# A two-layer graph network: layer 0's PSUM banks and query buffers lent to the last stretch of layer 1, and the tables of a batch group made four tiles further ahead

## The chip, the cores and the metric

The kernel runs on one core of a Trainium2 chip. The metric is the device time of one execution in microseconds. Before the change it is 2400.64 us, the median of three runs (2385.87 to 2404.24). The core has five instruction queues that run side by side: TensorE (PE, with its weight loads PEld), VectorE (DVE), ScalarE (ACT), GpSimd (POOL) and SyncE (SP). PE writes into PSUM[...]. POOL and SP mostly issue DMAs here: SP the plain ones, POOL those that gather or scatter rows by a list of indices.

## The reference, cut to what matters

x has 8 batches of 2048 nodes with 256 features; adj is a symmetric 0/1 matrix with about nine neighbours in a row, the node itself among them.

```
# layer 0: chunked attention, 4 heads of 64, chunks of 256 nodes
scores = clip(q . k / 8, -10, 10);  scores = -10 where adj == 0
attn   = softmax within each chunk;  ctx = attn @ v, summed over the 8 chunks
x = layernorm(x + LN(ctx @ Wo.T + x))
# layer 1: graph attention, 4 heads of 64
Wh = x @ W;  e = leaky_relu(s_src[i] + s_dst[j], 0.2), -inf where adj == 0
x = layernorm(x + elu(softmax(e over j) @ Wh))
```

Since adj has few ones, the kernel works on neighbour lists. Where adj is 0, a score in layer 0 is exactly -10, so all these together come to a constant part that the sum of v over a chunk supplies.

## The kernel before, in words

**Lists.** `edge_lists` reads adj in 16 tiles of 128 nodes, finds for each node its neighbours (at most 24), sorts all nodes by their number of neighbours, scatters the records in that order to `rec_d` (L118, POOL) and reads them back as `srt` (L122, SP). A tile of sorted nodes then needs as many slots as its largest node: `CAPS`, from 24 down to 5. `node`, `idx` and `valid` come out of `srt`. While it works, it calls `between(it)` after each tile of adj, which makes one table tile of batch group 0.

**Tables.** The 8 batches go in four groups g of two. `tables(g, t)` computes for 128 nodes of both batches k and v (into `kv_d[g]`, one DRAM row of 4 KB a node) and q (into `qx_d[g]`, beside x). Every second tile it loads two tiles of x (`load_x`, SP), transposes them on PE into `tk` banks (L336), copies them out with ACT, and hands the pair before to `add_beta` (POOL, L351, followed by SP's write to `qx_d`). Group g is complete after 16 table tiles, the last of which also makes the group's bias.

**Layer 0.** For tile t of group g, `fetch0` issues one indirect DMA on POOL for each slot: it gathers for each of the 128 nodes the `kv_d` row of its neighbour (L489). Two slots are a unit, and units come from a ring of 14 buffers (`RING`). Another gather brings `qx` (L527). `scores0` multiplies and sums, `softmax0` normalises, `context0` weights the v parts in place (L501 on DVE, L507 on ACT for a quarter of the units) and sums the slots on PE by transposing them into one PSUM bank `acc` (L514). `finish0` multiplies by Wo and applies both layernorms, and `rows1` makes layer 1's row (Wh and the logits of both batches) for `wh_d`.

**Layer 1** works on two groups together (p = 0 for groups 0 and 1, p = 1 for groups 2 and 3), so that its rows in `wh_d[p]` are 4160 bytes. `fetch1` gathers them, also through L489. `softmax1` (L680 to L700) needs all slots of the tile and leaves the weights in the SBUF tile `e`. `context1` weights both groups' parts in place (L501 and L507 again) and sums them into two `acc` banks, which ACT copies out (L722). `finish1` transposes back through the single `mf` bank (L734), applies elu (L737 to L741) and the layernorm, and leaves a `scatter` in the list `late`: for p = 0 one indirect DMA to `hold_d` (L748), for p = 1 four to the output (L753), which POOL issues when `scatters()` is called.

**Order.** `seq` is the order of all tiles, written out by hand: 32 tiles of layer 0 (groups 0 and 1), then two tiles of layer 0 (groups 2 and 3) for each tile of layer 1 with p = 0, and last the 16 tiles of layer 1 with p = 1, with nothing beside them. I call these the last stretch. In step k the loop first issues the gathers of step k + 1 (`fetch`), then the scatters, then scores, the earlier tiles' `rows1` and `finish0`, one table tile of the next group, and this tile's softmax and context. Before the first tile of a new group, `tables_first` holds the fetch back until the last table of that group has been made, because any row of the group may be gathered. The framework below places the instructions on each engine's queue in an order of its own near the written one, and puts in the waits. Each engine then works strictly in its queue's order.

**PSUM.** The eight banks are `acc` (2), `tk` (2), `tf` (2), `mf` (1) and `pr` (1). `tk`, `tf` and `pr` are used by layer 0 and its tables; `rows1` also takes `tf`. `qx` has four buffers in SBUF, and layer 1's `xr`, with the same size, two of its own.

Of the kernel before, what the change touches and what calls it, by code (L numbers as in the profile page):

```python
# [9 lines left out]
F32 = mybir.dt.float32  # L10
# [4 lines left out]
ALU = mybir.AluOpType  # L15
# [27 lines left out]

def edge_lists(tc: tile.TileContext, pool, bank, adj, const, ident, rec_d, B, between):

# [49 lines left out]
        between(it)  # L97


    rank = const.tile([P, NT], F32, name="rank")  # L100
    rank_i = pool.tile([P, NT], I32, name="rank_i")

    half = NT // 2
# [4 lines left out]
    for it in range(half):  # L108
        gt = pool.tile([P, N], F32, tag="v", name="v", bufs=2)
        nc.vector.tensor_scalar(gt, krow, key[:, it:it + 1], 0.0, op0=ALU.is_gt, op1=ALU.add,  # L110
                                accum_out=rank[:, it:it + 1])
        junk = pool.tile([P, N], BF16, tag="junk", name="junk", bufs=1)
        k = half + it
        nc.scalar.activation(junk, krow, AF.Sign, bias=nkey[:, k:k + 1], accum_out=rank[:, k:k + 1])
        nc.vector.tensor_scalar(rank[:, k:k + 1], rank[:, k:k + 1], 0.5, 0.5 * (N - 1), op0=ALU.mult, op1=ALU.add)
        nc.vector.tensor_copy(rank_i.rearrange("p (h t) -> p t h", h=2)[:, it], rank.rearrange("p (h t) -> p t h", h=2)[:, it])
        for k in (it, half + it):
            nc.gpsimd.indirect_dma_start(out=views[k],  # L118
                                         out_offset=bass.IndirectOffsetOnAxis(ap=rank_i[:, k:k + 1], axis=0),
                                         in_=rec[:, k, :], in_offset=None)  # L120
    srt = pool.tile([P, NT, REC], F32, name="srt")
    nc.sync.dma_start(srt, rec_d.rearrange("(t p) r -> p t r", p=P))  # L122

# [46 lines left out]
    return idx, valid, same, node, nodeb, rank, over  # L170


@with_exitstack
def sparse_path(ctx: ExitStack, tc: tile.TileContext, keep, x, adj, Wq, bq, Wk, bk, Wv, bv, Wo, bo, gamma, beta, W, a,
# [57 lines left out]
    def bank(tag, bufs=2):  # L232

        return ps.tile([P, 512], F32, tag=tag, name=tag, bufs=bufs)
# [182 lines left out]
        tables(0, t)  # L417


    rings, turn = [ctx.enter_context(tc.tile_pool(name="ring0", bufs=1))], [0]  # L420

    def unit():
# [8 lines left out]

    with tc.tile_pool(name="lists", bufs=1) as pool:
        with nc.allow_low_precision("exact small integers"):
            idx, valid, same, node, nodeb, rank, over = edge_lists(tc, pool, bank, adj, const, ident, rec_d, B,
                                                             first_tables)
        nc.vector.tensor_copy(keep, over)

    rings.append(ctx.enter_context(tc.tile_pool(name="ring1", bufs=1)))
# [57 lines left out]
    def weighted(part, al, s0, n):  # L496

        e = part.shape[2] // D
        pv = part.rearrange("p s (e d) -> p s e d", d=D)
        av = al[:, :, s0:s0 + n].rearrange("p e s -> p s e").unsqueeze(3).to_broadcast([P, n, e, D])  # L500
        nc.vector.tensor_tensor(pv, pv, av, op=ALU.mult)  # L501
# [165 lines left out]
        nc.sync.dma_start(wh_d[g // 2][t * P:(t + 1) * P, g % 2 * WW:(g % 2 + 1) * WW], wh)  # L667


    got1, st1 = {}, {}  # L670

    def fetch1(p, t):
# [2 lines left out]
    def softmax1(p, t):  # L675
        S = CAPS[t]
        units = got1[p, t]
        z = small.tile([P, 2, GH, S], F32, tag="z1", name="z1")
        for u, s0, n in units:
            nc.vector.tensor_tensor(z[:, :, :, s0:s0 + n].rearrange("p k e s -> p s k e"),  # L680
                                    u.rearrange("p s (k w) -> p s k w", k=2)[:, :, :, GF:GF + GH],
                                    sd[p % 2][:, t].unsqueeze(1).to_broadcast([P, n, 2, GH]), op=ALU.add)
# [12 lines left out]
        r = small.tile([P, 2 * GH], F32, tag="r", name="r")  # L695
        nc.vector.tensor_reduce(r, e, axis=AX.X, op=ALU.add)

        nc.vector.tensor_scalar(r, r, 1e-30, None, op0=ALU.max)
        nc.vector.reciprocal(r, r)
        nc.vector.tensor_tensor(e, e, r.unsqueeze(2).to_broadcast([P, 2 * GH, S]), op=ALU.mult)  # L700
        st1[p, t] = e

    def context1(p, t):
        S = CAPS[t]
        e = st1.pop((p, t))
        units = got1.pop((p, t))
        accs = [bank("acc").rearrange("p (c r) -> p c r", r=P) for _ in range(2)]
        na = len(units) // 4, (len(units) + 2) // 4
        for i, (u, s0, n) in enumerate(units):
            for k in range(2):  # L710
                if i >= len(units) - na[k]:
                    weighted_act(u[:, :, k * WW:k * WW + GF], e[:, k * GH:(k + 1) * GH], s0, n)
        for i, (u, s0, n) in enumerate(units):
            for k in range(2):
                part = u[:, :, k * WW:k * WW + GF]
                if i < len(units) - na[k]:
                    weighted(part, e[:, k * GH:(k + 1) * GH], s0, n)
# [6 lines left out]
        xr = work.tile([P, 2, GF], F32, tag="xr", name="xr")  # L724
        nc.sync.dma_start(xr, x1_d[p][t * P:(t + 1) * P])
        st1[p, t] = hTs, xr

    def finish1(p, t):
        hTs, xr = st1.pop((p, t))
        sums = small.tile([P, 2 * G], F32, tag="sums1", name="sums1")  # L730
        for k, hT in enumerate(hTs):
            ph = bank("mf", 1)
            for c in range(G * KC):
                nc.tensor.transpose(ph[:, c * P:(c + 1) * P], hT[:, c, :], ident)  # L734

# [551 lines left out]
```

## Time and profile before

| | |
|---|---|
| median of three runs | 2400.64 us (2385.87 to 2404.24) |
| profiled execution | 2397.55 us, its span 2395.8 us |
| PE, PEld busy | 1900.4 us (79%), 1622.0 us (68%) |
| DVE busy | 1833.5 us (77%) |
| ACT busy | 1409.0 us (59%) |
| POOL busy | 1505.0 us (63%) |
| DMA | 669.10 MB, mean 279 GB/s; indirect DMAs of POOL 505.01 MB |
| granted TensorE clock, mean | 0.885 |
| L489, POOL's gathers | 656 of `kv_d`, mean 1235 ns; 328 of `wh_d`, mean 1270 ns |

An engine's busy time counts its own work, not its waits, and not the time between two DMA issues. In a row of a group stand the line, the engine, the operation, what is written and read, the shapes, how often, then the busy time and the mean of one, and at last the engine's idle time just before these instructions, with what ended it. In a timeline a row has the start, the duration, the engine and the line, and in brackets the idle time before it and its releaser. PEclk is the share of full clock that PE was granted. Times within the execution are counted from the start of its span. By them, the lists and group 0's tables take the first 195 us, the first tile of layer 0 gathers from 195, and the last stretch gathers from 1994 to the end.

### The profile page before, as it was taken

What the parts mean: (1) busy time and instruction counts of PE and PEld (TensorE: products, weight loads), DVE (VectorE), ACT (ScalarE), POOL (GpSimd) and SP (SyncE); (2) the same over time, 40 slices, a digit from 0 to 9 for tenths busy, and PEclk for the clock granted to TensorE, in tenths of its full rate; (3) what the DMA queues carried; (4) which work ended last, traced back from release to release, by engine and by line L of the source; (5) the groups of instructions that cost most, each with busy time, mean ns of one, the idle gap of its engine ahead of it and who ended that gap; (6) DMA issues with size and microseconds to landing.
All of it is one profiled execution on the core that took longest, in us unless ns stands there. A gap on an engine that the chain in (4) does not pass through costs nothing. (4 is left out here: it accounts for less than half of the span.)

```text
span 2395.8 us, 38844 instructions
## 1 busy us (share of the span) xinstructions
PE 1900.4 (79%) x11946; PEld 1622.0 (68%) x11946; DVE 1833.5 (77%) x4099; ACT 1409.0 (59%) x5036; POOL 1505.0 (63%) x1230
## 2 busy tenths in 40 slices
PE   7686889889899898999988885888678786664764
PEld 5565677778778787777876774776566675554653
DVE  6864587877588988588988886887788887775775
ACT  4573455546566555655565665664356677665766
POOL 3125455672666676376668856774677685787883
PEclk9897899899999999999998997987878987877887
DMA  7737877795889798598879977896679896786884
GB/s 259 242 137 272 265 270 281 260 346 209 316 287 320 260 334 319 212 388 298 302 258 353 360 281 238 285 321 221 230 274 326 306 319 248 278 310 231 302 296 154
DMA packets 239982, 669.10 MB, mean 279 GB/s; under 512 B 43688, under 2 KB 70059, under 8 KB 237719
## 3 DMA queue, kind: packets, MB, share of 16 engines
q0 software_dynamic: 156800, 505.01, 60.1%
q1 hardware_dynamic: 79248, 151.55, 17.2%
q10 hardware_dynamic: 3718, 9.97, 1.3%
q8 instruction: 98, 1.61, 0.3%
q14 instruction: 118, 0.96, 0.1%
HBM read 612.79 MB, written 126.36 MB: 309 GB/s over the span
## 5 line engine op out<-in xcount | busy, mean ns | idle before, releaser
L489 POOL DMA_INDIRECT u<-kv_d,idx x656 | 810.2, 1235 | 436.4 <-PE acc L514 185.7
L514 PE MATMUL acc<-ident,u 128*128 128x128 f32 x5248 | 713.4, 291 | 157.0 <-DVE u L501 89.0
L514 PEld LDWEIGHTS acc<-ident,u 128*128 128x128 f32 x5248 | 637.5, 151 | 220.7 <-DVE u L501 133.2
L489 POOL DMA_INDIRECT u<-wh_d,idx x328 | 416.5, 1270 | 148.2 <-issue 76.4
L566 PE MATMUL pr<-ident,u 128*128 128x128 f32 (+1 forms) x1984 | 287.0, 295 | 78.7 <-DVE u L547 77.2
L501 DVE TENSOR_TENSOR u<-u,al 128x1024 f32<-128x1024 f32 x280 | 334.5, 1234 | 1.5
L566 PEld LDWEIGHTS pr<-ident,u 128*128 128x128 f32 (+1 forms) x1984 | 245.4, 151 | 110.8 <-DVE u L547 104.6
L547 DVE TENSOR_TENSOR u<-u,qx 128x1024 f32<-128x1024 f32 (+1 forms) x248 | 302.0, 1218 | 18.3 <-DMA u<-kv_d,idx 15.1
L501 DVE TENSOR_TENSOR u<-u,z 128x1024 f32<-128x1024 f32 x266 | 314.4, 1212 | 0.6
L507 ACT ACTIVATE u<-u,z 128x64 f32<-128x64 f32 x1008 | 262.0, 337 | 25.0 <-DVE z L700 17.1
L507 ACT ACTIVATE u<-u,al 128x64 f32<-128x64 f32 x800 | 209.1, 342 | 23.2 <-DVE al L607 22.3
L663 PE MATMUL mf<-wa,x1T 128*128 128x264 f32 x512 | 167.6, 455 | 23.1 <-ACT x1T L658 14.8
L351 POOL TENSOR_TENSOR xt<-xt,beta_r 128x1024 f32<-128x1024 f32 x32 | 77.1, 2410 | 143.1 <-PE tk L336 126.3
L385 PE MATMUL tk<-wq,xT 128*128 128x256 f32 x512 | 145.2, 397 | 24.4 <-ACT kvs L379 24.4
L451 ACT ACTIVATE nm<-sums 128x2 f32<-128x2 f32 (+1 forms) x160 | 32.4, 202 | 221.3 <-DVE sums L641 122.6
L372 PE MATMUL tk<-wkv,xT 128*128 128x256 f32 x512 | 151.7, 410 | 12.9 <-ACT xC L341 12.6
L635 PE MATMUL mf<-wo,cT 128*128 128x256 f32 x512 | 148.4, 415 | 6.3 <-ACT whs L666 5.3
L376 PE MATMUL tk<-wkv,xC 128*128 128x256 f32 x512 | 144.5, 399 | 0.0
L663 PEld LDWEIGHTS mf<-wa,x1T 128*128 128x128 f32 x512 | 101.7, 218 | 59.7 <-ACT x1T L658 23.6
L455 ACT ACTIVATE sq<-o,nm 128x256 bf16<-128x256 f32 x256 | 129.7, 507 | 5.3
L554 DVE TENSOR_TENSOR u<-u,qx 128x1024 f32<-128x1024 f32 (+1 forms) x96 | 116.0, 1214 | 16.6 <-DMA qx<-qx_d,node 7.1
L590 DVE TENSOR_SCALAR sc<-tf 128x64 f32<-128x64 f32 (+5 forms) x64 | 14.0, 218 | 138.2 <-PE tf L576 138.2
(168 smaller groups left out, 3254.0 us busy)
## 6 DMA issues: line engine op xcount, KB each, us to landing
kv_d<-kvs SPq DMA_DIRECT2D x48, 512.0 KB, 6.0
wh_d<-whs SPq DMA_DIRECT2D x64, 260.0 KB, 5.8
xt<-in_x_dram SPq DMA_DIRECT2D x64, 256.0 KB, 4.8
qx_d<-xt SPq DMA_DIRECT2D x32, 512.0 KB, 4.4
qx_d<-qs SPq DMA_DIRECT2D x64, 256.0 KB, 5.8
x_d<-o SPq DMA_DIRECT2D x64, 256.0 KB, 5.2
xr<-x_d SPq DMA_DIRECT2D x32, 512.0 KB, 4.9
u<-kv_d,idx POOLq DMA_INDIRECT x656, 6.5
```

The source lines that it names most:

```text
L372: nc.tensor.matmul(pm[:, 0:F], xT[:, b * KC + kc, rows], wkv[:, kc, 0:F], start=(kc == 0), stop=False, skip_group_check=True)
L376: nc.tensor.matmul(pm[:, F:], xC[:, b * KC + kc, rows], wkv[:, kc, F:], start=False, stop=(kc == KC - 1), skip_group_check=True)
L385: nc.tensor.matmul(qb, xT[:, b * KC + kc, rows], wq[:, kc, :], start=(b == 0 and kc == 0), stop=False, skip_group_check=True)
L455: nc.scalar.activation(sq, src[:, k, :], AF.Square, bias=nm[:, k:k + 1], accum_out=m2[:, k:k + 1])
L489: nc.gpsimd.indirect_dma_start(out=u[:, k, 0:width], out_offset=None, in_=table, in_offset=bass.IndirectOffsetOnAxis(ap=idx[:, t, s0 + k:s ...
L501: nc.vector.tensor_tensor(pv, pv, av, op=ALU.mult)
L507: nc.scalar.activation(pe, pe, AF.Copy, scale=al[:, e, s0 + k:s0 + k + 1])
L514: nc.tensor.matmul(acc[:, c, :], part[:, k, c * P:(c + 1) * P], ident, is_transpose=True, start=first and k == 0 and c == 0, stop=last and ...
L547: nc.vector.tensor_tensor(prod.rearrange("p k j (s w) -> p k j s w", w=W8), u[:, :, 0:GF].rearrange("p s (k j w) -> p k j s w", k=UNIT, w=W8),
L566: nc.tensor.matmul(pr[0:n * W8, k, :], prod[:, j // (NJ // UNIT), j % (NJ // UNIT), :], ident, is_transpose=True, start=(j == 0), stop=(j ...
L635: nc.tensor.matmul(po[:, b, :], cT[:, b * KC + kc, :], wo[:, kc, :], start=(b == 0 and kc == 0), stop=False, skip_group_check=True)
L663: nc.tensor.matmul(pw[:, 0:F + 2 * H], xT[:, b * KC + kc, :], wa[:, kc, :], start=(kc == 0), stop=(kc == KC - 1))
```

## The change

- **Tables further ahead.** A new `lead_tables` makes the first four table tiles of group 1. `edge_lists` calls it, through the new argument `behind`, after the records' scatter and before `srt` is read. In the loop, step i of layer 0 now makes the table tile i + 16 + 4 in place of i + 16. So the tables of the last group are written out by step 43 in place of 47. `tables_first` is dropped: the fetch is always the first thing in a step. `rank` is allocated earlier, since group 1's tables store it.
- **Weights in PSUM.** For p = 1 (`LAST`), `softmax1` writes the normalised weights `w` into a `tf` bank, for the units that DVE weights. The slots that ACT weights are still scaled in the SBUF tile `e`, by an instruction of their own. `context1` hands `w` to `weighted` (L501).
- **Banks.** For p = 1, every second tile sums into `mf` and `pr` in place of the two `acc`, and `finish1` transposes into `tk` in place of `mf`.
- **xr** takes `qx` buffers (four) for p = 1.
- **Scatters.** In the last stretch, from its second tile on, `scatters` leaves the newest scatter in the list for one step more.

```diff
+    LEAD = 4
+    def lead_tables():
+        for t in range(LEAD):
+            tables(1, t)
...
             nc.gpsimd.indirect_dma_start(out=views[k],
...
+    behind()
     srt = pool.tile([P, NT, REC], F32, name="srt")
...
+    LAST = NG // 2 - 1
...
-        nc.vector.tensor_tensor(e, e, r.unsqueeze(2).to_broadcast([P, 2 * GH, S]), op=ALU.mult)
-        st1[p, t] = e
+        first = 0
+        if p == LAST:
+            w = bank("tf")[:, 0:2 * GH * S].rearrange("p (e s) -> p e s", s=S)
+            nc.vector.tensor_tensor(w, e, r.unsqueeze(2).to_broadcast([P, 2 * GH, S]), op=ALU.mult)
+            first = UNIT * (len(units) - (len(units) + 2) // 4)
+        else:
+            w = e
+        if first < S:
+            nc.vector.tensor_tensor(e[:, :, first:], e[:, :, first:], r.unsqueeze(2).to_broadcast([P, 2 * GH, S - first]),
+                                    op=ALU.mult)
+        st1[p, t] = w, e
...
-        accs = [bank("acc").rearrange("p (c r) -> p c r", r=P) for _ in range(2)]
+        other = p == LAST and order.index(t) % 2
+        accs = [bank(*((("mf", 1), ("pr", 1))[k] if other else ("acc", 2))).rearrange("p (c r) -> p c r", r=P)
+                for k in range(2)]
...
-                    weighted(part, e[:, k * GH:(k + 1) * GH], s0, n)
+                    weighted(part, w[:, k * GH:(k + 1) * GH], s0, n)
...
+        if p == LAST:
+            xr = work.tile([P, 2, GF], F32, tag="qx", name="xr", bufs=4)
+        else:
+            xr = work.tile([P, 2, GF], F32, tag="xr", name="xr")
...
-            ph = bank("mf", 1)
+            ph = bank("tk") if p == LAST else bank("mf", 1)
...
-    def scatters():
-        for f in late:
-            f()
-        late.clear()
+    def scatters(keep=0):
+        while len(late) > keep:
+            late.pop(0)()
...
-        tables_first = layer == 0 and seq[k + 1][0] == 0 and seq[k + 1][1] % NT == 0
-        if not tables_first:
-            fetch(k + 1)
-        scatters()
+        fetch(k + 1)
+        scatters(int(layer == 1 and g == LAST and i > NT))
...
-            if g + 1 < NG:
-                tables(g + 1, i % NT)
-            if tables_first:
-                fetch(k + 1)
+            if i + NT + LEAD < NG * NT:
+                tables(*divmod(i + NT + LEAD, NT))
```

More of the change, by code (lines that the diff above doesn't have):

```diff
@@ L42, with edge_lists @@
 EMIN = 4.5399929762484854e-05
-def edge_lists(tc: tile.TileContext, pool, bank, adj, const, ident, rec_d, B, between):
+def edge_lists(tc: tile.TileContext, pool, bank, adj, const, ident, rec_d, rank, B, between, behind):
     nc = tc.nc
@@ L97, in edge_lists @@
         between(it)
-    rank = const.tile([P, NT], F32, name="rank")
     rank_i = pool.tile([P, NT], I32, name="rank_i")
@@ L169, in edge_lists @@
     nc.vector.tensor_copy(over, op)
-    return idx, valid, same, node, nodeb, rank, over
+    return idx, valid, same, node, nodeb, over
 @with_exitstack
@@ L417, in first_tables @@
         tables(0, t)
+    LEAD = 4
+    def lead_tables():
+        for t in range(LEAD):
+            tables(1, t)
+    rank = const.tile([P, NT], F32, name="rank")
     rings, turn = [ctx.enter_context(tc.tile_pool(name="ring0", bufs=1))], [0]
@@ L433, in sparse_path @@
         with nc.allow_low_precision("exact small integers"):
-            idx, valid, same, node, nodeb, rank, over = edge_lists(tc, pool, bank, adj, const, ident, rec_d, B,
-                                                             first_tables)
+            idx, valid, same, node, nodeb, over = edge_lists(tc, pool, bank, adj, const, ident, rec_d, rank, B,
+                                                             first_tables, lead_tables)
         nc.vector.tensor_copy(keep, over)
@@ L699, in softmax1 @@
         nc.vector.reciprocal(r, r)
-        nc.vector.tensor_tensor(e, e, r.unsqueeze(2).to_broadcast([P, 2 * GH, S]), op=ALU.mult)
-        st1[p, t] = e
+        first = 0
[9 more added lines that the diff above has]
+        st1[p, t] = w, e
     def context1(p, t):
         S = CAPS[t]
-        e = st1.pop((p, t))
+        w, e = st1.pop((p, t))
         units = got1.pop((p, t))
-        accs = [bank("acc").rearrange("p (c r) -> p c r", r=P) for _ in range(2)]
+        other = p == LAST and order.index(t) % 2
+        accs = [bank(*((("mf", 1), ("pr", 1))[k] if other else ("acc", 2))).rearrange("p (c r) -> p c r", r=P)
+                for k in range(2)]
         na = len(units) // 4, (len(units) + 2) // 4
@@ L723, in context1 @@
             hTs.append(hT)
-        xr = work.tile([P, 2, GF], F32, tag="xr", name="xr")
+        if p == LAST:
+            xr = work.tile([P, 2, GF], F32, tag="qx", name="xr", bufs=4)
+        else:
+            xr = work.tile([P, 2, GF], F32, tag="xr", name="xr")
         nc.sync.dma_start(xr, x1_d[p][t * P:(t + 1) * P])
```

## The prediction

> **What bounds the kernel now.** I read the page first (PE 79%, DVE 77%, POOL 63% of the span), saw that no engine bounds the whole, and asked for windows stage by stage. The columns are the stretch, its length, busy us of each engine, the granted clock, the DMA share and GB/s.
>
> ```profile
> core 0: us, PE busy (x) PEld busy (x) DVE busy (x) ACT busy (x) POOL busy (x), PEclk, DMA share, GB/s
> 160.00:360.00 200.00, 154.98 (x855) 129.01 (x854) 123.21 (x255) 96.46 (x306) 109.26 (x97) 0.84 0.74 248
> ...
> 540.00:620.00 80.00, 74.93 (x480) 63.39 (x477) 53.10 (x123) 49.16 (x186) 23.85 (x20) 1.00 0.56 196
> ...
> 1280.00:1400.00 120.00, 100.36 (x675) 86.09 (x675) 97.49 (x213) 75.46 (x278) 97.01 (x73) 0.93 0.95 355
> ...
> 2063.00:2348.00 285.00, 175.57 (x1188) 150.89 (x1188) 199.68 (x458) 188.46 (x679) 228.89 (x184) 0.81 0.78 285
> ```
>
> At the start (160 to 360) nothing is full: PE has 45 us to spare. At the first change of group (540 to 620) DMA falls to 0.56 and POOL all but stops, but PE is 94% busy. Around 1280 to 1400 DMA is at 0.95. In the last stretch no compute engine passes 70%, and POOL shows 80%. The groups of that stretch show what the 80% hides:
>
> ```profile
> L489 POOL DMA_INDIRECT u<-wh_d,idx x132 | 164.4, 1246 | 40.2 <-issue 26.5 <-PE acc L514 5.2 <-DVE u L501 3.4
> ...
> L501 DVE TENSOR_TENSOR u<-u,z 128x1024 f32<-128x1024 f32 x109 | 129.1, 1216 | 0.2
> ...
> L753 POOL DMA_INDIRECT out_dram<-xr,nodeb x52 | 64.5, 1240 | 19.3 <-issue 7.9 <-ACT xr L470 4.3 <-ACT u L507 2.4
> ...
> L738 DVE SCALAR_TENSOR_TENSOR xr<-mf,xr 128x512 f32<-128x512 f32 x22 | 15.1, 686 | 8.5 <-DMA xr<-x_d 5.1 <-ACT hT L737 3.4
> ```
>
> 132 + 52 = 184 indirect DMAs. Each is followed by 0.30 us, so 164.4 + 64.5 + 184 x 0.30 = 284 us of 285: POOL issues without a hole and **is** the bound there; who "released" each 0.30 us is chance. How long one issue takes is in the timeline of two moments of that stretch:
>
> ```profile
> 2191.34 0.24 DVE L680 TENSOR_TENSOR z<-u,sd 128x32 f32<-128x32 f32 x1 [2.85 <-DMA u<-wh_d,idx]
> 2191.53 0.99 POOL L489 DMA_INDIRECT u<-wh_d,idx  x1 [0.30 <-issue]
> 2192.83 1.00 POOL L489 DMA_INDIRECT u<-wh_d,idx  x1 [0.30 <-DMA u<-wh_d,idx]
> ...
> 2225.99 8.02 DVE L501 TENSOR_TENSOR u<-u,z 128x1024 f32<-128x1024 f32 x7
> 2226.04 2.03 POOL L489 DMA_INDIRECT u<-wh_d,idx  x1 [0.30 <-DVE u L501]
> ...
> 2228.38 1.97 POOL L489 DMA_INDIRECT u<-wh_d,idx  x1 [0.31 <-PE acc L514]
> ...
> 2230.65 1.96 POOL L489 DMA_INDIRECT u<-wh_d,idx  x1 [0.30 <-DVE u L501]
> ```
>
> With DVE idle an issue takes 0.99 us; under the multiplications of L501, whose two inputs lie in SBUF, it takes twice that. So DVE sets POOL's pace.
>
> **The last stretch, part by part.** The new factor w makes one input of L501 a PSUM bank in all of the last stretch (133 of the kernel's 266 such instructions). *What POOL gains.* [...] where an input is in PSUM the issue should fall to near 0.99. L680, L741 and the softmax still have two SBUF inputs. In 2050 to 2396 they are some 67 us (L741 24, L680 13, the softmax's lines about 30) against 147 of L501; the excess of 0.25 us on 184 issues, 46 us, shrinks to 67/214 of it, 14 us. That is 1.07 us an issue: 184 x 1.37 = 252 us. POOL gains 32[...].
>
> *What DVE pays.* L738 reads 512 elements from PSUM in 686 ns and L741 256 from SBUF in 410, a slope of 1.08 ns; 1024 elements would take 1239 against 1216. [...] 133 x 0.023 = 3 us by the row[...]. The scaling that stays in SBUF adds 16 small instructions of about 0.25 us (L699 at 128x16 takes 249 ns), 4 us. Both lie in the 85 us that DVE idles in the stretch[...].
>
> *What the stretch then waits for.* DVE needs 200 of 252, ACT 188, PE 176, DMA 0.78 x 285 = 222. All fit, but each tile's softmax needs all its rows landed (DVE waits 61 us at L680), and the ring holds 14 units of which the 24-row tile takes 12: PE idled 20.7 us there while 10 gathers came, and these saw an idle DVE already. So I take 26 of the 32.
>
> *The held-back scatter* removes waits of POOL for ACT's xr, behind which gathers stand: three holes of 3.2, 3.6 and 3.7 us before 2063. The first is not held back; I take 4 of 10. The waits of 13.4 and 8.3 at the end stay, since no gather is behind them. *Accumulators in mf and pr, transposes in tk, xr in the query buffers*: they lift waits of PE (L734 for DVE 37 us, L514 for L722) which POOL's pace covers today; 0, and without that cover they are what lets 26 be reached. Between 0 and 8 us. Last stretch: -30.
>
> **The tables, part by part.** One table tile holds PE from 154.8 to 161.0, 6.2 us, plus half of its pair's 8 transposes (L336), 0.6; ACT 268/64 = 4.2 us. The built order of ACT shows 5 to 6 tables ahead of each context where there were 1 to 2, so the change does what it says. *Front:* some 3.5 more tables come before tile 5 of group 0: 24 us of PE. PE idles 45 us in 160 to 360, partly in places that the in-order queue can't use. POOL now has add_beta of pair 0 in front of the first gather (its transposes ended at 195.1, the gather began at 195.2: +2.4) and that of pair 2 after nine gathers instead of 29; the gathers behind would wait for PE, but they waited for the ring's zeroing until 214 anyway. SP has the x loads and qx_d writes of the pairs behind these. Between 0 and +34; I take +12.
> *Changes of group:* the fetch no longer stands behind the last table.
>
> ```profile
> 580.89 2.42 POOL L351 TENSOR_TENSOR xt<-xt,beta_r 128x1024 f32<-128x1024 f32 x1 [16.23 <-issue]
> 610.09 1.01 POOL L489 DMA_INDIRECT u<-kv_d,idx  x1 [26.78 <-DMA qx_d<-qs]
> ```
>
> POOL's 43 us go (and 44 at 970), but PE was 94% busy, so what returns is PE's 5 us there plus some of the 6 us that it idles in the refill at DMA 1.01 (620 to 660). 0 to 20 each; I take 7. Third change: PE idled 14 us at 1473; 0 to 14, I take 7. *Tiles 43 to 47* lose four tables, 27 us of PE and some 5 MB (256 + 512 + 256 + 256 KB a tile; 14 us at 355 GB/s). The stretch is bound by DMA; 14 is what DMA alone gives, between 0 and 27; I take 13. Tables: +12 - 14 - 7 - 13 = -22.
>
> **Sum.** 2397.55 (span 2395.8) - 30 - 22 = 2345.5 for the profiled execution. That one lies 3.1 below the median of the runs, 2400.64; I state 2348.
>
> **The rivals.**
> *Both parts in full* (0.20). POOL at 0.99 gives 46 + 8, boundaries and tiles 43 to 47 give 40 with the front free: 2397.55 - 94 + 3 = 2307. For: POOL's row has no hole. Against: DVE would run at 84%, DMA at 93% with a 14-unit ring.
> *The pace goes to landing* (0.20). POOL issues faster, but softmax waits for rows and units free no sooner: the tail gives 10 and its scatter 2, the tables 5, because PE at 94% was the bound at the changes of group. 2384. For: PE's 94%, L680's 61 us. Against: at 2186 to 2198 one issue in 1.30 us was followed by landings at that pace.
> *Slower: reading PSUM is dear* (0.09). If a multiplication with its factor repeated from PSUM ran at half pace, 2.43 us, DVE would need 200 + 109 x 1.22 = 333 us in the stretch, more than its 285: DVE is the bound, +63 with some slack, +10 for the 24 others, tables -22: 2452. It decides from 200 + 109 x d = 285, d = 0.78, so 2.0 us an instruction. Against: L738's 686 ns.
> The likeliest case has 0.51, and 2325 to 2372 as its own range.
>
> **Chances and range.** About 1% (24 us) is what a measurement of this kernel tells from no change. Faster: 0.49 of the likeliest, the full case's 0.20, 0.05 of the landing case: 0.74. Same: 0.17, slower: 0.09. Leaving 0.1 at each end gives 2306 to 2392.
>
> **What would show it.** In the changed profile: L489 and L753 of the last stretch at 1.05 to 1.1 us, and the run of 184 issues 25 to 32 us shorter; multiplications out of tf at 1.22 to 1.28 us; POOL's holes of 26.8 and 24.4 us gone, with DMA above 0.75 in those places while PE stays near 94%; the first cT copy (247.4 before) 5 to 20 us later; PE below 80% busy where tiles 43 to 47 are. The prediction is wrong if issues stay near 1.24 us although L501 has one PSUM input, if DVE becomes full in the last stretch, or if the delay of the first tiles is still there at 1400.

## The result, and the profile after

The changed kernel takes 2349.84 us, the median of four runs (2340.43 to 2373.87), against 2393.26 us of the kernel before (2377.1 to 2404.24): a ratio of 0.986, 95% interval 0.982 to 0.990. Here and below a ratio compares only runs that did not fall into the slower of two states, so it can differ a little from the quotient of two medians. The profiled execution has a span of 2350.7 us where before had 2395.8, so 45.1 us are to be found between the two traces. They are easily divided: the gathers of the last stretch began at 1993.8 us before and begin at 1998.0 now, so everything ahead of the last stretch is 4 us *longer*, and the last stretch went from 402 to 353 us, 49 *shorter*. The prediction had -22 and -30 for the two.

The windows that were shown of before, now of after (stretch, its length, busy us of each engine, the granted clock, the DMA share, GB/s); the last is again the part of the last stretch in which POOL shows no hole:

```profile
core 0: us, PE busy (x) PEld busy (x) DVE busy (x) ACT busy (x) POOL busy (x), PEclk, DMA share, GB/s
160.00:360.00 200.00, 164.47 (x939) 139.52 (x940) 122.60 (x253) 100.62 (x327) 112.38 (x97) 0.89 0.77 266
540.00:620.00 80.00, 72.98 (x457) 61.55 (x456) 62.98 (x136) 44.31 (x169) 47.52 (x38) 0.97 0.86 299
1280.00:1400.00 120.00, 99.12 (x639) 85.08 (x637) 102.14 (x217) 67.38 (x240) 92.55 (x72) 0.87 0.94 340
2067.00:2305.00 238.00, 168.07 (x1192) 154.60 (x1192) 198.10 (x466) 187.28 (x672) 178.73 (x177) 0.82 0.89 330
```

PE has more to do at the start (164.5 of 200 us, 155.0 before), the first change of group no longer empties POOL (47.5 of 80 us, 23.9 before; DMA 0.86, 0.56 before), and in the last stretch DMA rose from 0.78 to 0.89 while DVE does the same 198 us of work in 47 us less. The groups of that stretch (line, engine, operation, names and shapes, count, busy us and mean ns, idle time before with what ended it):

```profile
L500 POOL DMA_INDIRECT u<-wh_d,idx x125 | 127.5, 1020 | 42.8 <-issue 26.1 <-PE acc L525 4.3 <-DMA u<-wh_d,idx 3.4
L512 DVE TENSOR_TENSOR u<-u,tf 128x1024 f32<-128x1024 f32 x108 | 126.2, 1210 | 0.0
L784 POOL DMA_INDIRECT out_dram<-xr,nodeb x52 | 51.9, 998 | 16.8 <-issue 8.4 <-DMA u<-wh_d,idx 2.3 <-ACT u L518 1.6
L769 DVE SCALAR_TENSOR_TENSOR xr<-tk,xr 128x512 f32<-128x512 f32 x23 | 15.5, 686 | 4.8 <-ACT hT L768 4.7
```

An issue takes 1.02 and 1.00 us where it took 1.25 and 1.24. 177 x 0.30 + 127.5 + 51.9 = 232 of the 238 us: POOL still issues almost without a hole and still sets the pace, only faster (the window holds 177 of the DMAs, the one of before 184). L512 with its factor in PSUM takes 1210 ns, and took 1216 with both inputs in SBUF. The timeline (start, us, engine, line, and in brackets the idle time before) at a moment under a run of multiplications, as the one shown of before was:

```profile
2116.91 4.61 DVE L512 TENSOR_TENSOR u<-u,tf 128x1024 f32<-128x1024 f32 x4
2117.09 1.04 POOL L500 DMA_INDIRECT u<-wh_d,idx  x1 [0.30 <-DVE xr L772]
2118.44 1.02 POOL L500 DMA_INDIRECT u<-wh_d,idx  x1 [0.30 <-issue]
2119.77 1.00 POOL L500 DMA_INDIRECT u<-wh_d,idx  x1 [0.30 <-issue]
2121.07 1.00 POOL L500 DMA_INDIRECT u<-wh_d,idx  x1 [0.30 <-issue]
```

Four issues under the multiplications take 1.00 to 1.04 us; at the moment shown of before they took 1.96 to 2.03. That moment was one of the worst: of all 52 issues of before's last stretch that lay at least nine tenths under a multiplication, 41 took over 1.1 us, and the mean is 1.63. After the change 94 lie so under a multiplication with its factor in PSUM; their mean is 1.00 and the longest took 1.04. Nine multiplications, of layer 1 with p = 0, still read both inputs from SBUF in the same trace, and the four issues under them have a mean of 1.65.

POOL's timeline around the first change of group, where it stood for 43 us before:

```profile
582.32 0.97 POOL L538 DMA_INDIRECT qx<-qx_d,node  x1 [5.50 <-DVE o L658]
583.60 1.00 POOL L500 DMA_INDIRECT u<-kv_d,idx  x1 [0.30 <-issue]
...
602.65 0.96 POOL L538 DMA_INDIRECT qx<-qx_d,node  x1 [4.50 <-DVE idx L492]
603.64 2.36 POOL L352 TENSOR_TENSOR xt<-xt,beta_r 128x1024 f32<-128x1024 f32 x1
606.15 1.00 POOL L500 DMA_INDIRECT u<-kv_d,idx  x1 [0.16 <-issue]
```

The long hole is gone. In its place stand waits of some 5 us ahead of `qx` gathers.

Layer 0 writes one cT per tile, 64 in all, so their times show where the 4 us came from: the cT copy of the changed kernel against that of before, in us (positive is later).

| tile | 0 | 15 | 17 | 22 | 24 | 31 | 33 | 41 | 48 | 63 |
|---|---|---|---|---|---|---|---|---|---|---|
| after | +6.4 | +6.0 | -4.3 | +17.8 | +1.5 | +11.1 | +4.4 | +23.0 | +8.0 | +4.1 |

The front is later (+6). The changes of group (15 to 17, 31 to 33) gain 10 and 7, and tiles 41 to 48 gain 15. But between them the changed kernel falls behind: 15 us from tile 17 to 31 and 19 from 33 to 41. The prediction has nothing for these.

Not all of it is time gained or lost, since the same work can stand on the other side of a mark. By the matmuls of k and v on PE, eight of a kind for each table tile, the changed kernel makes half a table less than before between tiles 15 and 17 and one less between 31 and 33, and one more in each of the stretches 17 to 31 and 33 to 41. With the 6.8 us of PE that the prediction reckoned for a table, and if PE's work sets the pace there, an estimate is that the changes of group gained nearer 7 and 0 us, and that the stretches between lost nearer 8 and 12.

### The profile page after: what moved, and what is told of

Read it like the earlier page. It is cut to its first block, busy times and chain, and to the rows that moved or that the text cites. A ratio compares the mean times of both kernels' runs of the same rounds, so it can differ in the third digit from the quotient of the medians.

```text
span 2350.7 us, 38793 instructions
## 1 busy us (share of the span) xinstructions
PE 1876.9 (80%) x11946; PEld 1621.3 (69%) x11946; DVE 1835.3 (78%) x4115; ACT 1410.2 (60%) x5036; POOL 1446.9 (62%) x1230
## 5 line engine op out<-in xcount | busy, mean ns | idle before, releaser
L500 POOL DMA_INDIRECT u<-kv_d,idx x656 | 795.0, 1212 | 415.7 <-PE acc L525 232.2
L525 PE MATMUL acc<-ident,u 128*128 128x128 f32 x4624 | 618.2, 289 | 133.8 <-DVE u L512 119.3
L525 PEld LDWEIGHTS acc<-ident,u 128*128 128x128 f32 x4624 | 555.3, 150 | 179.7 <-DVE u L512 149.2
L500 POOL DMA_INDIRECT u<-wh_d,idx x328 | 384.9, 1173 | 144.3 <-issue 62.9
L512 DVE TENSOR_TENSOR u<-u,al 128x1024 f32<-128x1024 f32 x280 | 334.2, 1226 | 1.1
L558 DVE TENSOR_TENSOR u<-u,qx 128x1024 f32<-128x1024 f32 (+1 forms) x248 | 294.5, 1188 | 49.3 <-DMA u<-kv_d,idx 47.7
L518 ACT ACTIVATE u<-u,z 128x64 f32<-128x64 f32 x1008 | 262.8, 337 | 31.5 <-DVE z L724 31.5
L386 PE MATMUL tk<-wq,xT 128*128 128x256 f32 x512 | 144.9, 404 | 27.8 <-ACT kvs L380 27.8
L512 DVE TENSOR_TENSOR u<-u,z 128x1024 f32<-128x1024 f32 (+1 forms) x133 | 157.3, 1211 | 0.2
L512 DVE TENSOR_TENSOR u<-u,tf 128x1024 f32<-128x1024 f32 x133 | 154.8, 1206 | 0.0
L373 PE MATMUL tk<-wkv,xT 128*128 128x256 f32 x512 | 146.1, 401 | 8.9 <-ACT xC L342 8.6
L538 POOL DMA_INDIRECT qx<-qx_d,node x64 | 76.0, 1188 | 122.5 <-DVE o L658 52.5
L565 DVE TENSOR_TENSOR u<-u,qx 128x1024 f32<-128x1024 f32 (+1 forms) x96 | 115.6, 1206 | 38.9 <-DMA qx<-qx_d,node 22.1
```

Of the source, the lines that this page charges most:

```text
L373: nc.tensor.matmul(pm[:, 0:F], xT[:, b * KC + kc, rows], wkv[:, kc, 0:F], start=(kc == 0), stop=False, skip_group_check=True)
L386: nc.tensor.matmul(qb, xT[:, b * KC + kc, rows], wq[:, kc, :], start=(b == 0 and kc == 0), stop=False, skip_group_check=True)
L500: nc.gpsimd.indirect_dma_start(out=u[:, k, 0:width], out_offset=None, in_=table, in_offset=bass.IndirectOffsetOnAxis(ap=idx[:, t, s0 + k:s ...
L518: nc.scalar.activation(pe, pe, AF.Copy, scale=al[:, e, s0 + k:s0 + k + 1])
L525: nc.tensor.matmul(acc[:, c, :], part[:, k, c * P:(c + 1) * P], ident, is_transpose=True, start=first and k == 0 and c == 0, stop=last and ...
L558: nc.vector.tensor_tensor(prod.rearrange("p k j (s w) -> p k j s w", w=W8), u[:, :, 0:GF].rearrange("p s (k j w) -> p k j s w", k=UNIT, w=W8),
```

## The experiments

### The two halves

The first three take the change apart. *Tables alone*, on the changed kernel:

```diff
-        if p == LAST:                      # both places
+        if False:
...
-        other = p == LAST and order.index(t) % 2
+        other = False
...
-            ph = bank("tk") if p == LAST else bank("mf", 1)
+            ph = bank("mf", 1)
...
-        scatters(int(layer == 1 and g == LAST and i > NT))
+        scatters()
```

> The kernel before with the tables' part of the change alone; the last stretch is that of before. The profiles of before and after put the start of the last stretch's gathers at 1993.8 and 1998.0. Theory 'the lead gives nothing' (PE, 94% busy at the changes of group, takes back there what POOL no longer waits): the time stays within 0.3% of before, the last stretch is still some 402 us long and its 184 issues are at 1.24 us. Theory 'the lead gives 22 us and the after profile hides it by chance' (the prediction's step): 0.9% faster, a ratio of 0.991.

Measured: 2410.9 us against 2385.94, a ratio of 1.010 (1.006 to 1.013). The last stretch takes 406 us. So the lead doesn't give nothing, and it doesn't give 22 us: it costs 23 (14 to 31 by the interval). Both theories fall. (2385.94 us is the kernel before, measured again beside these four runs.)

*The last stretch alone*, on the changed kernel:

```diff
-                                                             first_tables, lead_tables)
+                                                             first_tables, lambda: None)
...
-        fetch(k + 1)
+        tables_first = layer == 0 and seq[k + 1][0] == 0 and seq[k + 1][1] % NT == 0
+        if not tables_first:
+            fetch(k + 1)
...
-            if i + NT + LEAD < NG * NT:
-                tables(*divmod(i + NT + LEAD, NT))
+            if g + 1 < NG:
+                tables(g + 1, i % NT)
+            if tables_first:
+                fetch(k + 1)
```

> The changed kernel without the tables' part: its order and its held fetch at a change of group are those of before, the last stretch has all its edits. Theory 'the lead gives nothing': ratio 0.980 to 0.983 to before, that is 2345 to 2352, the same as the changed kernel or a few us less; last stretch 350 to 355 us long. Theory 'the lead gives 22 us': ratio 0.987 to 0.99, some 20 us slower than the changed kernel.

Measured: 2335.09 us, a ratio of 0.981 (0.977 to 0.985), below the changed kernel's 0.986, with the last stretch at 352 us. Its time is 10 us below the range of the theory that the lead gives nothing, but its ratio is inside that theory's 0.980 to 0.983, since the kernel before was faster here too. So this run speaks against a lead that gives 22 us, and does not by itself tell one that costs from one that gives nothing. The profiles do: the last stretch begins to gather at 1998.0, 2006.0 and 2007.6 us in the three kernels with the lead (changed, weights in SBUF, tables alone), and at 1976.2, 1981.7 and 1993.8 in the three without it (this one, the weights in PSUM alone, before).

*Weights back in SBUF*, all else as in the changed kernel (`if p == LAST` ahead of `w = bank("tf")` becomes `if False`):

> The changed kernel with the weights of the last stretch left in SBUF; banks, query buffers and the held scatter stay. Theory 'a second SBUF input of DVE slows POOL's issue': issues in the last stretch go back from 1.01 to 1.22 to 1.27 us, the stretch from 353 to 390 to 402 us, the time to 2385 to 2400. Rival 'banks and buffers opened the stretch, and the issue follows from shorter queues': the issue stays below 1.1 us and the time within 10 us of the changed kernel.

Measured: 2398.28 us, a ratio of 1.004 (1.002 to 1.006), with the stretch at 394 us and a mean issue of 1.25 us, as the theory of the second SBUF input had it; the rival falls. *Weights in PSUM as the only edit of before* (the lines that matter):

```diff
...
+        if p == LAST:
+            w = bank("tf")[:, 0:2 * GH * S].rearrange("p (e s) -> p e s", s=S)
+            nc.vector.tensor_tensor(w, e, r.unsqueeze(2).to_broadcast([P, 2 * GH, S]), op=ALU.mult)
+            first = UNIT * (len(units) - (len(units) + 2) // 4)
...
-                    weighted(part, e[:, k * GH:(k + 1) * GH], s0, n)
+                    weighted(part, w[:, k * GH:(k + 1) * GH], s0, n)
```

> The kernel before with the weights of the last stretch in a tf bank as the only edit. Theory 'the PSUM operand is nearly all': issues at 1.0 to 1.05 us, the last stretch 355 to 365 us long instead of 402, ratio 0.981 to 0.985. Rival 'without banks and buffers PE and DVE waits take the place of POOL': issues at 1.0 to 1.05 us too, but holes between them, the stretch 375 to 390 us long, ratio 0.990 to 0.995.

Measured: 2350.83 us, a ratio of 0.987 (0.983 to 0.991), between the ranges of the two theories, and a stretch of 365 us, at the upper end of the first one's range: the PSUM operand is most of the gain, not nearly all. POOL's groups over the whole last stretch show the two halves of it, first of the kernel with the weights in SBUF and all other edits, then of the one with the weights in PSUM and no other edit:

```profile
L500 POOL DMA_INDIRECT u<-wh_d,idx x164 | 197.0, 1201 | 67.5 <-issue 32.3 <-DMA wh_d<-whs 12.5 <-PE acc L525 8.3
L784 POOL DMA_INDIRECT out_dram<-xr,nodeb x64 | 87.7, 1371 | 36.9 <-ACT xr L481 19.2 <-issue 7.3 <-DVE u L512 3.0
```

```profile
L500 POOL DMA_INDIRECT u<-wh_d,idx x164 | 168.4, 1027 | 67.6 <-issue 45.7 <-PE acc L525 10.1 <-DVE u L512 2.4
L784 POOL DMA_INDIRECT out_dram<-xr,nodeb x64 | 64.4, 1006 | 54.6 <-ACT xr L481 39.4 <-issue 6.1 <-ACT u L518 2.4
```

The issue time follows where L512's factor lies, whether or not banks are lent: 1.20 and 1.37 us from SBUF with all banks lent, 1.03 and 1.01 from PSUM with none (before, from SBUF with none, 1.24 and 1.23). The windows of the last stretch, one kernel a fence: tables alone, weights in SBUF, weights in PSUM only, all edits without the lead.

```profile
2008.00:2414.00 406.00, 248.30 (x1666) 215.84 (x1664) 275.67 (x677) 270.06 (x946) 289.11 (x232) 0.79 0.72 259
```

```profile
2006.00:2400.00 394.00, 241.03 (x1668) 219.33 (x1666) 275.11 (x679) 270.59 (x946) 289.90 (x232) 0.77 0.73 262
```

```profile
1982.00:2347.00 365.00, 242.64 (x1667) 212.43 (x1665) 276.48 (x693) 269.46 (x946) 237.58 (x232) 0.81 0.79 288
```

```profile
1976.00:2328.00 352.00, 231.13 (x1668) 209.63 (x1667) 275.62 (x695) 270.57 (x946) 238.63 (x232) 0.83 0.80 293
```

The lead doesn't touch this stretch: it is 402 us without any edit (406 with the tables alone) and 352 with all edits (353 with the tables). From 402 or 406 to 394 and from 365 to 352, the banks, the buffers and the held scatter are worth 8 to 13 us with either place of the weights. From 402 or 406 to 365 and from 394 to 352, the PSUM operand is worth 37 to 42. POOL has 232 DMAs with 0.30 us each behind them, 70 us; so its holes are 406 - 289 - 70 = 47 us without the other edits and 394 - 290 - 70 = 34 with them, and in PSUM 365 - 238 - 70 = 57 and 352 - 239 - 70 = 43. What the other edits take away are POOL's holes. The largest that shrank is POOL's wait for ACT's xr ahead of a scatter: 39.4 us with the PSUM weights alone, 24.7 with all edits. Which of the other edits did it was not separated.

### What the lead loses by

In the tables-alone kernel tile 22 is 24.7 us late and tile 41 31.5, and much the same is seen in the changed kernel, so the pattern isn't chance. The waits of POOL and ACT differ between the kernel before and the changed one in many places; three grew by some 40 us or more. Before (engine, what waited, for what: us in total, times, longest):

```profile
POOL u L489 <- PE acc L514: 220.3, 104, 16.9
...
POOL qx L527 <- DVE al L607: 18.9, 3, 10.4
POOL qx L527 <- DVE o L647: 17.1, 3, 8.5
...
ACT pl L479 <- DMA u<-kv_d,idx: 10.5, 9, 2.9
```

After:

```profile
POOL u L500 <- PE acc L525: 270.3, 111, 14.6
...
POOL qx L538 <- DVE o L658: 52.5, 11, 8.7
POOL qx L538 <- DVE ebuf L608: 34.8, 7, 8.7
...
ACT pl L490 <- DMA u<-kv_d,idx: 50.3, 23, 6.4
```

The first row is POOL's wait for a free unit of the ring, which PE empties; it grew by 50 us, while POOL's two holes at the changes of group went away, so part of its waiting only moved. The other two I took for the suspects. Counted over the trace, with waits over 0.5 us, 8 `qx` gathers waited 47 us before and 21 wait 110 us now. A qx buffer is one of four and comes free with `finish0`, and the gathers behind it on POOL wait too. In the built order of before, most qx gathers stood right behind their own tile's gathers; in the neighbourhood of the 24-row tile they stood ahead. After the change it stands three to six gathers late in tiles 17 to 19, and three to ten early in tiles 21 to 23, ahead of its own tile's last rows. No line of the diff says so: the framework finds another order for the changed program. In the same way it moves the copies of `places`, which only group 1 has, ahead on ACT to where their rows have not landed.

*All qx gathers in the written order*, with the lead and without it (the changed kernel and the last stretch alone):

```diff
+                if width < 2 * WW and last_qx:       # a kv_d gather stays behind the qx gather before it
+                    tc.add_manual_dep(ins.ins, last_qx[-1].name, mybir.DependencyInfo(
+                        mybir.DependencyClass.NoSync, mybir.DependencyReason.DATA), reason="after qx")
...
-        nc.gpsimd.indirect_dma_start(out=qx, ...)
+        ins = tc.keep_in_program_order(
+            nc.gpsimd.indirect_dma_start(out=qx, ...))
+        last_qx.append(ins.ins)
```

> The changed kernel, but each tile's qx gather is pinned in POOL's queue behind the kv_d gathers of its own tile and ahead of those of the next; nothing else differs. In the changed kernel 21 qx gathers wait 110 us in all for a free qx buffer with other gathers queued behind them (8 and 47 us before), most of them in tiles 16 to 23 and 32 to 39, where the framework put them up to 22 gathers ahead of their place. Theory 'the order of qx in POOL's queue ate the lead's gain': these waits fall below 60 us, the cT copies of tiles 18 to 22 and 35 to 41 no longer fall behind, and the time is 15 to 30 us below the changed kernel: 2318 to 2335, ratio 0.973 to 0.98. Rival 'tables further ahead are dear in themselves' (PE and ACT do them ahead of the work in hand): within 6 us of the changed kernel, ratio 0.983 to 0.988.

> Control: the kernel with the last stretch's edits alone (no lead), with the same pins on qx. There the qx gathers lie in place already but for tiles 8 to 11, 24 to 27 and 39 to 43. Theory 'order of qx': those few cost little, 2325 to 2338, ratio 0.977 to 0.981, and the lead with pins is faster than this by 5 to 20 us. Rival 'tables further ahead are dear in themselves': this stays the faster by some 15 us.

Measured: 2469.33 us with the lead (ratio 1.036, 1.034 to 1.039), 2458.66 without (1.032, 1.029 to 1.034). Both theories missed by over 100 us: I had taken the written place for the harmless one. The 24-row tile needs 24 of the ring's 28 slots, so a qx gather behind all its rows comes when the ring is nearly full, and DVE's first products need it. DVE's wait in the pinned kernel without the lead, which without the pins waits 8.7 us there in all:

```profile
DVE u L572 <- DMA qx<-qx_d,node: 81.8, 15, 11.9
```

What the pair still tells, since POOL's order of qx is the same in both: with the lead minus without it, the cT copies are at +15.4 (tile 0), +27.8 (15), +23.1 (17), +41.0 (22), +40.4 (33), +28.5 (41), +10.4 (48). From 33 to 41 the lead now *gains* 12 us where it lost 19 in the changed kernel. That fits a loss that came from the order of qx, but is weak: there the pinned kernel without the lead itself falls 38 us behind the kernel before, which may hide the lead's loss. From 17 to 22 it still loses 18. That is group 1, where ACT waits 74.1 us for the rows of `places` in the kernel with the lead and 39.0 in the other.

*The cause alone*: no lead, each qx gather ahead of its own tile's gathers (the pins as above, with the qx gather written first in `fetch0`).

> The suspected cause alone: the kernel with the last stretch's edits and no lead, but each qx gather pinned ahead of its own tile's kv_d gathers. Theory 'order of qx': POOL stands at qx for over 150 us in all, and the time rises by 20 to 60 us over the 2335 of the last stretch's edits alone, ratio 0.99 to 1.005. Rival 'waiting at qx is covered, since PE bounds layer 0': within 8 us of 2335, ratio 0.978 to 0.984.

Measured: 2361.4 us, 26 us above the 2335 of the same kernel without the pins; the two come from different chips, but their ratios, 0.991 (0.988 to 0.995) and 0.981 (0.977 to 0.985), do not overlap. 22 qx gathers wait 154 us. So waits at qx are not all covered by PE. These pins put every qx gather 5 to 24 places ahead of the end of its own tile's gathers, which is not the order of the changed kernel. It is not the same everywhere: up to tile 8 this kernel was 25 us *ahead* of the one without pins, and lost 64 from there to tile 48.

### Keeping the orders

The runs came from several chips. The first four experiments ran on one that the record calls 10, the next three on 15; the kernel before takes 2386 and 2384 us there. The last five ran on chips 8 (three runs) and 9 (two), where it takes 2584 and 2583 us; only their ratios and what they show beside each other can be used. Three kernels keep ACT's order, POOL's order, or both, on the changed kernel. ACT's:

```diff
-            nc.scalar.copy(pl[:, s0:s0 + n], u[:, :, 2 * GF])
+            tc.keep_in_program_order(nc.scalar.copy(pl[:, s0:s0 + n], u[:, :, 2 * GF]))
```

> The changed kernel, with only the copies of `places` (the ranks that ACT takes out of group 1's gathered rows) pinned in ACT's queue behind what is written before them. In the changed kernel ACT waits 50 us at them for gathers to land (10 before), and prT, x1T and whs copies that PE waits for stand behind; tiles 18 to 22 fall 17 us behind. Theory 'ACT is blocked at the copies of places': its waits there go below 15 us, tiles 18 to 22 no longer fall behind, the time is 10 to 17 us below the changed kernel: 2332 to 2340, ratio 0.977 to 0.981. Rival 'the blocked copies only show that gathers land late': within 5 us of the changed kernel.

POOL's (QX_AT lists, for each qx gather, the number of kv_d gathers ahead of it in the built order of before; `pin` is the dependence of the diff further up):

```diff
+                if width < 2 * WW:
+                    queries()               # issues the qx gathers that are due here, pinned
...
-        qx = work.tile([P, 2 * GF], F32, tag="qx", name="qx", bufs=4)
-        nc.gpsimd.indirect_dma_start(out=qx, ...)
+        queries()
+        qx = got_q.pop((g, t))
```

> The changed kernel, with each qx gather pinned at the place among the kv_d gathers that it has in POOL's queue before the change. (Pinning all of them behind their own tile cost 110 us with and without the lead, so that run couldn't tell.) Theory 'the order of qx ate the lead's gain': waits at qx fall from 110 to about 50 us, the tiles of group 2 no longer fall behind, 10 to 25 us below the changed kernel: 2325 to 2340, ratio 0.974 to 0.981. Rival 'the order of PE and ACT decides, not POOL's': within 6 us of the changed kernel, ratio 0.982 to 0.987.

Both:

> Both pins of the two runs above on the changed kernel. If the two orders are what the lead lost by, it now gives what the prediction's step said, 10 to 22 us against the last stretch's edits alone: 2313 to 2325, ratio 0.969 to 0.974. If only one of them counts, 2330 to 2340. If neither, 2345 to 2352.

Measured: places 2561.94 us, 0.992 of before (0.989 to 0.995); qx 2565.23, 0.994 (0.991 to 0.997); both 2555.16, 0.983 (0.977 to 0.988). Both pins together are ahead of either alone here, though the interval of the repeat below meets both others, so how the gain divides between them stays open. All three ratios are above the ranges expected of them. With neither the changed kernel nor the last stretch alone on this chip, that doesn't tell what the pins are worth.

What was expected of the waits can be judged. With the copies of `places` pinned, ACT's waits for their rows are gone (0 us; below 15 was expected). With qx pinned, the trace has the order of before, gather for gather, and still 18 qx gathers wait 166 us, where about 50 were expected; with `places` alone pinned, on the same chip and with the changed kernel's order of qx but for six gathers, 21 wait 154. So the order among the gathers is not what makes these waits. 107 of the 166 us lie at tiles 16 to 20 and 32 to 36, right behind the changes of group where the fetch is no longer held. Hence the last two:

> The kernel with both pins (places and qx) on the changed kernel, again, since the three runs before came from a chip on which the kernel before takes 2584 us, and neither the changed kernel nor the last stretch's edits alone was measured there. On that chip both pins gave 0.983 of before, the places pin alone 0.992, the qx pin alone 0.994. Theory 'the lead is worth its 22 us once POOL's and ACT's orders are kept': 10 to 22 us below the last stretch's edits alone on the same chip. Rival 'the pins only take back what the lead cost': within 8 us of them. Third, 'the lead costs 10 us at the front and through layer 0 whatever the orders': 8 to 15 us above them.

> The last stretch's edits alone, again, on the chip of the run above: ratio 0.977 to 0.985 to before, the level that the kernel with both pins is compared with. By 'the lead is worth its 22 us' this one is the slower of the two by 10 to 22 us, by 'the pins only take back' they are equal within 8 us, by 'the lead costs whatever the orders' this one is the faster by 8 to 15 us.

Measured, both on chip 9: both pins 2552.23 us, 0.986 (0.978 to 0.993); the last stretch alone, the same kernel that had 0.981 on chip 10, 2598.39, 1.005 (1.002 to 1.008). The lead with its orders kept is 46 us faster than no lead, twice what "it is worth its 22 us" expected, and the theory that it costs whatever the orders falls for this chip. Whether the lead without the pins would do as well here is not known: with one pin it had 0.992 and 0.994 on chip 8, which is also below 1.005. The cT copies say where: from tile 14 to 17 the kernel with both pins gains 30 us on the one without the lead, from 29 to 32 16, from 41 to 48 26. The first two are changes of group, where the fetch was held, and the last holds the third one and the tiles that have no table left beside them. So the held fetch is dearer on this chip: without the lead, tiles 15 to 17 take 71.7 us, and 52.0 in the same kernel on chip 10. At the front the lead loses 10 (tile 2). Between the changes of group it now loses nothing: tiles 17 to 22 take 117 us with both pins and 118 without the lead, tiles 33 to 41 take 257 and 256. With one pin, on chip 8, the first of these stretches takes 138 us (`places`) and 129 (qx).

Against that, the last stretch's edits give nothing on this chip, going by the time (1.005); the kernel before has no profile there. The window without the lead:

```profile
2160.00:2596.00 436.00, 256.51 (x1674) 231.14 (x1672) 279.04 (x699) 274.64 (x950) 238.38 (x232) 0.75 0.67 237
```

436 us where the same kernel took 352, with POOL's 238 us unchanged (its gathers at 1033 ns, 1035 on chip 10) and the clock at 0.75 for 0.83. POOL no longer sets the pace. PE had half its clock for 768 of the 2577 us that the record of the clock covers, 457 of 2307 on chip 10. In this trace ACT stands still for 219 us in all, DVE for 24 and PE for 10 with nothing recorded to end it, and 0 on chip 10; no landing of a DMA is recorded in the traces of chips 8 and 9. What holds the stretch is open.

So of the versions measured no one is the best on all chips: on chip 10 it is the last stretch alone (0.981), on chips 8 and 9 the changed kernel with both pins (0.983 and 0.986). The changed kernel on chips 8 and 9 and the one with both pins on chips 10 and 15 were not measured.

## Why the prediction was right, and where it wasn't

The predicted 2348.0 lies 1.8 us from the median of 2349.84. It is right by two errors that cancel: the traces have -49 and +4 where it has -30 and -22. That it lies so near is luck. As a ratio it said 0.978, below the measured interval (0.982 to 0.990): the kernel before, with one more run, came to 2393 us instead of the 2401 that it started from.

**The last stretch's bound: right.** POOL's issues set its pace, DVE's second SBUF input set POOL's, and the PSUM operand takes that away. With only the place of the weights changed, the mean issue is 1.25 us from SBUF (the third experiment) and 1.03 from PSUM (the changed kernel). So the case in which the edit gains nothing, with issues that stay near 1.24 us, is out.

**"I take 26 of the 32": mis-sized.** It measured 37 to 42 us. Two terms made the 32 too small. The excess over 0.99 us an issue that was put down to the other DVE instructions with two SBUF inputs, 14 us, is about 4 (177 x 0.024): the mean issue fell to 1.01 instead of 1.07. And only 184 of the 232 DMAs were counted: over all of them POOL's busy time went down by 48 us (286 to 239). The 6 us put off for rows that have not landed were about right: 48 less 37 to 42 did not reach the stretch, though DVE's wait for rows at the logits fell from 63.6 us to 11.3.

**Held scatter "4 of 10", banks "0, between 0 and 8": mis-sized.** Together 8 to 13 us, not 4.

**DVE's price: right.** 1210 ns against 1216; the trace showed not even the row's 23 ns. The second scaling is 17 instructions of 207 ns, 3.5 us for the 4 reckoned.

**"Tables: +12 - 14 - 7 - 13 = -22": the step that failed.** Its own terms came out in part. The front is +6.4 in the changed kernel and +11.5 in the tables-alone kernel for +12. The first two changes of group read -10 and -7 for -14, by the estimate above nearer -7 and 0. The third and tiles 43 to 47 give -15 (tile 41 to 48) for -20. But the sum leaves out what the lead does to every tile between: 15 us lost in group 1 and 19 in group 2, by the estimate 8 and 12. The working looked at the tables' own place on ACT ("5 to 6 tables ahead of each context") and on POOL (add_beta), and took the order of the rest as given. That order moved: qx gathers on POOL, copies of `places` on ACT. By the runs' times the lead costs 23 us without the last stretch's edits, and some 15 with them (2349.84 against 2335.09, ratios 0.986 and 0.981 with intervals that overlap).

That these two orders are the cause is not shown; what the lead loses by stays open. For it: the waits, the 26 us of early qx gathers alone, and that with both pins the stretches between the changes of group take no longer than without the lead (117 and 257 us on chip 9). Against it: with the order of qx kept as it was before, the waits at qx stayed (166 us), and with ACT's waits at `places` gone, tiles 17 to 22 still took 138 us. The lead without pins is missing on chips 8 and 9, and the pinned lead on chip 10. A rival that no run separates is the clock: from tile 33 to 41 PE had half its clock for 31, 34 and 31 us in the three kernels with the lead (changed, weights in SBUF, tables alone), and for 7, 10 and 20 in the three without. Its matmuls took 214 us there in the changed kernel and 203 before. From 17 to 22 the clock was the same in both (7 us at half), so there it explains nothing.

**What would show it wrong.** "The delay of the first tiles is still there at 1400": a delay was there (tile 45, +15.0), and the tables' part had failed, but not as the sign meant it. The delay of the first tiles was gone by tile 17 (-4.3); the one at 1400 arose behind it. The others: issues at 1.02 and 1.00 us (1.05 to 1.1 expected), multiplications at 1.21 (1.22 to 1.28), both POOL holes gone with DMA at 0.86 in the first of those places, the first cT 6.4 us later (5 to 20), and PE at 77% from tile 43 to 47 (below 80).

**The rivals.** "Both parts in full" (2307) had the last stretch nearly right, at -54. "The pace goes to landing" (2384) had the wrong place, but its reason for the tables, PE at 94% at the changes of group, did not decide the time: what came of the gain there was lost elsewhere. "Reading PSUM is dear" (2452) falls: a multiplication with its factor in PSUM took 1210 ns, where this case needed 2.0 us.

## What to carry to other kernels

When a queue of DMA issues is the bound, ask what the engines beside it read: here one operand of DVE in PSUM, at no price to DVE (1210 ns a multiplication, 1216 before), gave 37 to 42 us on chip 10. When a wait is lifted in a kernel that a framework orders, look for where the waiting went: POOL's two holes of 43 and 44 us at the changes of group gave way to waits for the ring and for qx buffers, and the kernel became slower (a ratio of 1.010 with the tables alone). The built order of every queue is one thing to compare, but a changed order beside a longer wait is no proof: with the order put back, the waits at qx stayed. And a gain measured on one chip may be absent on the next (the last stretch alone: 0.981 on chip 10, 1.005 on chip 9), so versions are compared on the same one.

## What was not expected of the hardware

- Nearly the whole excess of an indirect DMA's issue went with one operand: a mean of 1.00 us, at most 1.04, under multiplications with a PSUM factor, and a mean of 1.63, up to 2.08, with both inputs in SBUF.
- A DVE multiplication of 128x1024 with one input in PSUM took 1210 ns, 1216 with both in SBUF.
- Chips differ by 8% on the same kernel (2386 us on chip 10, 2583 on chip 9), and the effect of the last stretch's edits from -1.9% to +0.5%, with the granted clock of that stretch at 0.83 and 0.75.
